# Last part of a four-layer graph network: three of four batches scaled by a product with a diagonal matrix, and the stores moved from GpSimd to SyncE

## The chip, the cores and the metric

The program runs on one core of a Trainium2 chip. A core has five engines that work side by side and meet at semaphores: TensorE (PE in the profile; its weight loads are listed as PEld), VectorE (DVE), ScalarE (ACT), GpSimd (POOL) and SyncE (SP), which here only starts transfers. SBUF is the working memory with 128 partitions; PSUM is the small memory of eight banks into which TensorE writes, one bank being 512 float32 values in each partition. The metric is the device time of one execution in microseconds, and the number that counts is the median of the runs.

## The reference

The program computes four graph layers on `x`, 128 graphs of 128 nodes and 256 features in float32. Each layer is followed by a residual sum and a layer norm. Only the last layer matters here:

```
A_hat = D^-1/2 (adj + I) D^-1/2
agg   = A_hat applied to x, for each of the 128 graphs
h     = relu(batchnorm(agg @ W1.T + b1))          # 512 wide
out   = batchnorm(h @ W2.T + b2)                  # 256 wide
x     = layernorm(x + out)                        # mean and variance over the 256 features, eps 1e-5
```

The batch norms take their mean and variance over all 128 x 128 nodes, so the second one can be applied only when the whole of `h @ W2.T` is there. Applying it is one scale and one shift for each feature. What follows is the residual sum and the layer norm, then the result is stored.

## The kernel before, in words

The 128 graphs are taken in 32 quads of four (`QB` is 4, `NQ` is 32). A quad of the layer's input `x` is kept in DRAM (`x3_dram`), laid out with nodes in the partitions. A quad of `h @ W2.T` stays in SBUF (`outs[q]`, shown as `agg`), and lies the other way round: features in the partitions, in two halves `o` of 128, and in the free dimension four batches of 128 nodes. The two have to be brought together, so the features-first data is turned by TensorE.

The order in which each engine executes its instructions is the order in which the program issues them; the whole part is inside a hand-written schedule, no planner reorders it. [...] Waits come from the data: an instruction waits for what it reads, and for the readers of what it overwrites.

`finish` ends the pass before: it aggregates the statistics of the second batch norm, computes its scale `sc2` and shift `sh2` (L1483 to L1495), applies both to the first quad (`halves`, L1497), and spreads them into two small matrices (`spread`, L1354 and L1355): `diag2`, a diagonal matrix with the scale, and `wide`, with the shift.

The last part (L1522 to L1602) is a software pipeline over the quads. One turn of its loop, for the number `q`, issues in this order:

- `moments(q, 0)`: the first half of quad `q` on VectorE. It adds the turned batches 0 and 1 to `x` in SBUF (L1554), and takes the layer norm's statistics of both (L1557, L1559).
- `scaled(q + 1)`: the next quad's turning. Batches 0 and 1 are scaled and shifted by ScalarE in place (`halves`, L1350, 256 columns for each feature half) and then transposed by TensorE into the PSUM bank `pt[0]` (L1537). Batches 2 and 3 go another way: a product with `diag2` turns and scales them at once into the bank `pt[1]` (L1545), the shift is added to `x` by GpSimd beforehand (L1542), and a product with the identity adds this `x` to the same bank (L1547). So for these two the residual sum is formed in PSUM and VectorE has no add.
- `coefficients(q - 1)`: two small instructions of VectorE that make the reciprocal `rs` (L1564) and minus the mean times `rs`, called `nm` (L1565).
- `apply(q - 1)`: four activations on ScalarE (L1577), one for each batch, which write the normed rows into SBUF; batches 0 and 1 are read from SBUF, 2 and 3 from PSUM. Then the store of the quad, issued by GpSimd (L1583). In the last quad VectorE takes two of the four (L1574), and SyncE and ScalarE store one half each (L1580, L1581).
- the load of a later quad of `x` on SyncE (`load_x3`, L1528).
- `moments(q, 1)`: statistics of batches 2 and 3, read from PSUM, and the square root on ScalarE (L1601).

Twelve buffers hold the quads of `x` (`NB` is 12). Eleven loads are issued ahead of the loop; in turn `q` the load of quad `q + 10` follows, into the buffer of quad `q - 2`, when that quad's store is through. A bank pair `pt` is used again after four quads.

Of the kernel before, what the change touches and what calls it, by code (L numbers as in the profile page):

```python
# [11 lines left out]
AF = mybir.ActivationFunctionType  # L12
# [14 lines left out]
def gnn_stack(ctx: ExitStack, tc: tile.TileContext, x, adj, w_qv_t, a, w_out_t, src, dst,  # L27
# [14 lines left out]
    nc = tc.nc  # L42
    B, N, D = x.shape
    H, DH = a.shape
    E = src.shape[0]
    P = 128
# [3 lines left out]
    QB = 4  # L50
    NQ = B // QB
# [10 lines left out]
    def ctile(shape, name, dtype=F32, pool=const):  # L62
        return pool.tile(shape, dtype, tag=name, name=name)

    def ps(name):
        return psum.tile([P, 512], F32, tag="ps", name=name)
# [6 lines left out]
    ident = ctile([P, P], "ident")  # L73
# [8 lines left out]
    sc2, sh2 = ctile([P, DC], "sc2"), ctile([P, DC], "sh2")  # L82
# [46 lines left out]
    with ExitStack() as phase:  # L129
# [556 lines left out]
        def layer2(k, b, room=None):  # L686
# [84 lines left out]
            pos = [ps("po2").rearrange("p (t d) -> p t d", d=D) for _ in range(2)]  # L771
            yield
            scaled(0)
            v.p4()
            yield
            v.p3()
            po = mix(0)
            scaled(1)
            yield
            mv = norm(0, po)  # L780
# [102 lines left out]
        bias = ctile([P, D], "bias", pool=cst2)  # L883
# [435 lines left out]
    with ExitStack() as phase:  # L1319
# [9 lines left out]
        def buf(name, tag="zbuf"):  # L1329
            return bufs.tile([P, 2 * QB * N], F32, tag=tag, name=name, bufs=NZ if tag == "zbuf" else NT)  # L1330
# [14 lines left out]
        diag2 = ctile([P, DC, P], "diag2", pool=cst)  # L1345
        shift_bc = ctile([P, D], "shift_bc", pool=cst)
        wide = ctile([P, DC, P], "wide", pool=cst)

        def halves(q, o, ag):
            nc.scalar.activation(ag[:, o, :2 * N], ag[:, o, :2 * N], AF.Identity, bias=sh2[:, o:o + 1],  # L1350
                                 scale=sc2[:, o:o + 1])

        def spread(o):
# [3 lines left out]
        with tc.manual_schedule(engines=None):  # L1357
# [114 lines left out]
            def finish(d):  # L1472

                last = ps("x3p")
                product(last, s4, d.b22, True)
                product(d.y, a22, d.t[3], False)
                ag = outs[d.q + 1][:, 0, :]
                nc.vector.tensor_add(ag, last, d.u2)
                nc.vector.bn_stats(st2[:, 0, d.q + 1, :], ag)
                t = bn_t[:, K3:K3 + DC]  # L1480

                def over(o):
                    nc.vector.bn_aggr(t[:, o, 0:2], st2[:, o].rearrange("p q s -> p (q s)"))  # L1483

                over(0)
                nc.vector.bn_stats(st2[:, 1, d.q, :], d.y)
                over(1)
                nc.scalar.activation(t[:, :, 2], t[:, :, 1], AF.Sqrt, bias=eps)
                for o in range(DC):
                    b = bn2[:, 0, o:o + 1]  # L1490
                    nc.vector.tensor_scalar(t[:, o, 3:4], t[:, o, 0:1], b, b, op0=ALU.add, op1=ALU.subtract)
                nc.vector.reciprocal(t[:, :, 2], t[:, :, 2])
                nc.vector.tensor_mul(sc2, bn2[:, 1], t[:, :, 2])
                nc.vector.tensor_mul(t[:, :, 3], t[:, :, 3], sc2)
                nc.vector.tensor_sub(sh2, bn2[:, 2], t[:, :, 3])  # L1495
                for o in range(DC):
                    halves(0, o, outs[0])  # L1497
                nc.scalar.copy(outs[d.q][:, 1, :], d.y)
                for o in range(DC):
                    spread(o)  # L1500
# [21 lines left out]
            x3s, sums, mvs, coefs = {}, {}, {}, {}  # L1522

            NB = NZ + NT

            def load_x3(q):
                x3s[q] = buf(f"x3l{q}", "zbuf" if q % NB < NZ else "tbuf").rearrange("p (b d) -> p b d", b=QB)
                nc.sync.dma_start(x3s[q], x3_dram[q].rearrange("p (b d) -> p b d", b=QB))  # L1528

            def scaled(q):  # L1530
                ag = outs[q]
                pt = [ps("pt3").rearrange("p (b d) -> p b d", d=D) for _ in range(2)]
                for o in range(DC):
                    if q > 0:
                        halves(q, o, ag)
                    for j in range(2):
                        nc.tensor.transpose(pt[0][:, j, o * P:(o + 1) * P], ag[:, o, j * N:(j + 1) * N], ident)  # L1537
                if q == 0:
                    pr = ps("shift_ps")[:, :D]
                    nc.tensor.matmul(pr, ones, wide.rearrange("p o n -> p (o n)"), start=True, stop=True)  # L1540
                    nc.scalar.copy(shift_bc, pr)
                nc.gpsimd.tensor_add(x3s[q][:, 2:, :], x3s[q][:, 2:, :], shift_bc.unsqueeze(1).to_broadcast([P, 2, D]))  # L1542
                for j in range(2):
                    for o in range(DC):
                        nc.tensor.matmul(pt[1][:, j, o * P:(o + 1) * P], ag[:, o, (j + 2) * N:(j + 3) * N], diag2[:, o, :],  # L1545
                                         start=(j == 0 and o == 0), stop=False, skip_group_check=True)
                nc.tensor.matmul(pt[1], ident, x3s[q][:, 2:, :], start=False, stop=True, skip_group_check=True)  # L1547
                sums[q] = pt

            def moments(q, half):  # L1550
                if half == 0:
                    mvs[q] = wk.tile([P, QB, 2], F32, tag="mv3", name="mv3", bufs=3)
                    moments.st = wk.tile([P, QB, 6], F32, tag="st3", name="st3", bufs=2)
                    nc.vector.tensor_add(x3s[q][:, :2, :], x3s[q][:, :2, :], sums[q][0])  # L1554
                src_ = x3s[q][:, :2, :] if half == 0 else sums[q][1]
                for t in range(2):
                    nc.vector.bn_stats(moments.st[:, 2 * half + t, :], src_[:, t, :])  # L1557
                for t in range(2):
                    nc.vector.bn_aggr(mvs[q][:, 2 * half + t, :], moments.st[:, 2 * half + t, :])  # L1559

            def coefficients(q):
                rs = wk.tile([P, QB], F32, tag="rs3", name="rs3", bufs=2)
                nm = wk.tile([P, QB], F32, tag="nm3", name="nm3", bufs=2)
                nc.vector.reciprocal(rs, coefs[q])  # L1564
                nc.vector.scalar_tensor_tensor(nm, mvs[q][:, :, 0], -1.0, rs, op0=ALU.mult, op1=ALU.mult)  # L1565
                coefs[q] = (rs, nm)

            def apply(q):
                rs, nm = coefs[q]
                o_q = out[q * QB:(q + 1) * QB].rearrange("b n d -> n b d")  # L1570
                for i in range(QB):
                    src_ = x3s[q][:, i, :] if i < 2 else sums[q][1][:, i - 2, :]
                    if q == NQ - 1 and i < 2:
                        nc.vector.tensor_scalar(x3s[q][:, i, :], src_, mvs[q][:, i, 0:1], rs[:, i:i + 1],  # L1574
                                                op0=ALU.subtract, op1=ALU.mult)
                    else:
                        nc.scalar.activation(x3s[q][:, i, :], src_, AF.Identity, bias=nm[:, i:i + 1],  # L1577
                                             scale=rs[:, i:i + 1])
                if q == NQ - 1:
                    nc.sync.dma_start(o_q[:, :2], x3s[q][:, :2, :])  # L1580
                    nc.scalar.dma_start(o_q[:, 2:], x3s[q][:, 2:, :])  # L1581
                else:
                    nc.gpsimd.dma_start(o_q, x3s[q])  # L1583

            for q in range(NB - 1):
                load_x3(q)
            scaled(0)
            for q in range(NQ + 1):
                if q < NQ:
                    moments(q, 0)  # L1590
                if q + 1 < NQ:
                    scaled(q + 1)
                if q > 0:
                    coefficients(q - 1)
                    apply(q - 1)
                    if q + NB - 2 < NQ:
                        load_x3(q + NB - 2)
                if q < NQ:
                    moments(q, 1)
                    sd = wk.tile([P, QB], F32, tag="sd3", name="sd3", bufs=2)  # L1600
                    nc.scalar.activation(sd, mvs[q][:, :, 1], AF.Sqrt, bias=eps)  # L1601
                    coefs[q] = sd  # L1602
# [44 lines left out]
```

## Time and profile before

| | |
|---|---|
| median of 9 runs | 3127.83 us (3124.24 to 3130.04) |
| the profiled execution | 3127.5 us |
| its span, first to last instruction | 3125.8 us |
| mean granted TensorE clock | 0.997 |
| busy over the span: TensorE, VectorE, ScalarE, GpSimd | 98%, 74%, 44%, 21% |
| the last part, from the first `halves` to the end of the span | 3013.83 to 3125.8 us |

The profile is one execution. Times are counted from the start of its span. A busy share over the whole span is an average of stages with different limits, so a stage is read by its own windows. In the lists of groups a row gives the line of the kernel, the engine and operation, what it writes and reads, how often, the busy time, the mean of one in nanoseconds, and the idle time of that engine just before, with what ended it. A 512-wide float32 product appears as two records for one matmul of the program, and so do the 128-wide ones with `diag2`; the transposes appear as one.

### The profile page before, as it was taken

The page shows a single profiled execution, that of the slowest core. Times are in us where ns is not written, and L with a number is a line of the kernel's source. Part 1 is how long each engine was busy: PE and PEld are TensorE (multiplying, and loading weights), DVE is VectorE, ACT ScalarE, POOL GpSimd, SP SyncE. Part 2 cuts the span into 40 slices and gives each one's busy share as a digit, 9 for nine tenths or more (in the row PEclk, how much of TensorE's full clock was granted, in tenths as well). Part 3 has the DMA queues.
Part 4 walks back from the last instruction along what each step waited for, and adds up shares of the span by engine and source line. Part 5 has one row for each costly group of instructions (what it writes and reads, how often), then busy time and mean ns, then how long its engine had stood idle before and what let it go on. Part 6 is the DMA issues. An engine that isn't in the chain of part 4 may idle for free. (4 is left out here: it accounts for less than half of the span.)

```text
span 3125.8 us, 39833 instructions
## 1 busy us (share of the span) xinstructions
PE 3075.7 (98%) x14800; PEld 2402.9 (77%) x14800; DVE 2312.7 (74%) x4599; ACT 1374.4 (44%) x2547; POOL 651.6 (21%) x536
## 2 busy tenths in 40 slices
PE   8899999999999999999999999999999999999997
PEld 4688888888888888888888888888888887874444
DVE  8777777777777777777777777777777776457888
ACT  3344443344444444433344444444333444326668
POOL 3311112222211111122222121111222220001135
PEclk9999999999999999999999999999999999999999
DMA  5633233333333332333333333323333331005557
GB/s 181 161 102 92 79 94 109 100 104 109 109 100 84 108 94 77 94 109 102 102 109 109 102 84 107 96 76 94 109 102 102 109 109 42 21 27 202 175 194 278
DMA packets 117473, 340.05 MB, mean 109 GB/s; under 512 B 14880, under 2 KB 51616, under 8 KB 108960
## 3 DMA queue, kind: packets, MB, share of 16 engines
q0 software_dynamic: 44688, 148.40, 19.6%
q1 hardware_dynamic: 70832, 188.18, 17.0%
q8 instruction: 118, 1.93, 0.3%
q10 hardware_dynamic: 1760, 0.92, 0.1%
q14 instruction: 75, 0.61, 0.1%
HBM read 252.00 MB, written 85.46 MB: 108 GB/s over the span
## 5 line engine op out<-in xcount | busy, mean ns | idle before, releaser
L580 PE MATMUL ph<-m,w 128*128 128x256 f32 x2048 | 473.1, 379 | 0.0
L660 PE MATMUL p<-w,h 128*128 128x256 f32 x2048 | 462.8, 379 | 0.0
L580 PEld LDWEIGHTS ph<-m,w 128*128 128x128 f32 x2048 | 386.8, 190 | 77.9 <-issue 14.8
L660 PEld LDWEIGHTS p<-w,h 128*128 128x128 f32 x2048 | 388.9, 190 | 66.4 <-issue 7.9
L336 POOL DMA_INDIRECT zs<-qd,src_idx x120 | 116.3, 969 | 1366.4 <-DMA qd<-qt 1331.5
L580 PE MATMUL ph<-m,w_s 128*128 128x256 f32 x1536 | 357.7, 379 | 0.4 <-DVE h L592 0.4
L580 PEld LDWEIGHTS ph<-m,w_s 128*128 128x128 f32 x1536 | 291.7, 190 | 53.6 <-issue 14.8
L336 POOL DMA_INDIRECT zs<-qd,dst_idx x120 | 189.3, 1577 | 338.8 <-DMA zs<-qd,src_idx 330.0
L586 ACT COPY u<-ph 128x512 f32<-128x512 f32 x128 | 74.6, 583 | 355.0 <-PE ph L580 355.0
L418 POOL DMA_INDIRECT attd<-at,att_idx x128 | 139.9, 1093 | 340.1 <-DMA attd<-at,att_idx 253.3
L596 ACT ACTIVATE h<-h 128x512 f32<-128x512 f32 x192 | 121.0, 630 | 138.8 <-DVE h L592 138.8
L113 ACT ACTIVATE ln_sd<-ln_mv,eps 128x2 f32<-128x2 f32 x192 | 55.9, 291 | 276.4 <-DVE ln_mv L108 276.4
L368 DVE SCALAR_TENSOR_TENSOR zs<-zs 128x1024 f32<-128x1024 f32 x125 | 151.3, 1210 | 8.0 <-DMA zs<-qd,dst_idx 5.3
L370 DVE TENSOR_TENSOR zs<-zs,a_bc 128x1024 f32<-128x1024 f32 x125 | 153.1, 1225 | 4.3
L371 DVE TENSOR_REDUCE scores<-zs 128x16 f32<-128x1024 f32 x125 | 152.5, 1220 | 4.3
L723 ACT COPY x2k<-y 128x384 f32<-128x384 f32 x192 | 91.8, 478 | 143.2 <-PE y L716 113.0
L106 DVE BATCH_NORM_STATS2 ln_st<-xr 128x6 f32<-128x256 f32 x384 | 144.5, 418 | 6.6
L121 DVE TENSOR_SCALAR xr<-xr,ln_mv,ln_rs 128x256 f32<-128x256 f32 x384 | 142.0, 412 | 7.0
L592 DVE TENSOR_TENSOR h<-ph,u 128x512 f32<-128x512 f32 x128 | 86.9, 680 | 71.9 <-PE ph L580 54.6
L437 ACT COPY adc<-ad 128x512 f32<-128x512 f32 x125 | 132.8, 1064 | 8.8 <-DMA ad<-attd 8.8
L684 POOL TENSOR_TENSOR xb<-xr,bias 128x512 f32<-128x512 f32 x64 | 99.1, 1549 | 150.8 <-DVE xr L121 143.7
L537 PE MATMUL pm<-wt_t,h 128*128 128x128 f32 x1024 | 126.9, 277 | 0.0
(359 smaller groups left out, 6083.6 us busy)
## 6 DMA issues: line engine op xcount, KB each, us to landing
ad<-attd SPq DMA_DIRECT2D x32, 1024.0 KB, 4.9
zd<-z SPq DMA_DIRECT2D x31, 1024.0 KB, 7.5
zl<-zd SPq DMA_DIRECT2D x62, 512.0 KB, 3.6
xr<-in_x_dram SPq DMA_DIRECT2D x32, 512.0 KB, 7.2
x3d<-xr SPq DMA_DIRECT2D x32, 512.0 KB, 2.6
x3l<-x3d SPq DMA_DIRECT2D x32, 512.0 KB, 5.5
out_dram<-x3l POOLq DMA_DIRECT2D x31, 512.0 KB, 5.8
xg<-in_x_dram SPq DMA_DIRECT2D x29, 512.0 KB, 3.8
```

The lines of the kernel that those rows point to most:

```text
L106: nc.vector.bn_stats(st[:, i, :], r[:, i, :])
L121: nc.vector.tensor_scalar(r[:, i, :], r[:, i, :], mv[:, i, 0:1], rs[:, i:i + 1], op0=ALU.subtract, op1=ALU.mult)
L336: nc.gpsimd.indirect_dma_start(out=s.z[c], out_offset=None, in_=s.qd, in_offset=bass.IndirectOffsetOnAxis(ap=idx[:, c:c + 1], axis=0), com ...
L368: nc.vector.scalar_tensor_tensor(z, z, SLOPE, z, op0=ALU.mult, op1=ALU.max)
L370: nc.vector.tensor_mul(z3, z3, a_bc.unsqueeze(1).to_broadcast([P, QB, D]))
L371: nc.vector.reduce_sum(s.es[:, c, :], z.rearrange("p (r d) -> p r d", d=DH), axis=AX.X)
L418: nc.gpsimd.indirect_dma_start(out=ad, out_offset=bass.IndirectOffsetOnAxis(ap=att_idx[:, c:c + 1], axis=0), in_=s.at[:, c, :], in_offset= ...
L437: (copy or nc.scalar.copy)(s.adc[:, j * H:(j + 1) * H, :], s.ad.rearrange("p (s r) -> p r s", r=R)[:, j * H:(j + 1) * H, :])
L537: nc.tensor.matmul(pm[:, c // 2, c % 2, :], quads[k].h1[i, c], wt_t, start=True, stop=True)
L580: nc.tensor.matmul(bank[g][:, i].rearrange("p b n -> p (b n)"), wa[:, c, f:f + P], s.m2[:, blk_b, c].rearrange("p b n -> p (b n)"), start= ...
L596: nc.scalar.activation(h, h if src_ is None else src_, AF.Relu)
L660: nc.tensor.matmul(p3[:, t * D:(t + 1) * D], s.h2[f // 2][:, f % 2, j + t, :], w3_sb[:, f, :], start=(f == 0), stop=(f == K2 - 1))
```

## The change

Of each quad, ScalarE scales and shifts only batch 0 and TensorE transposes only batch 0. Batches 1, 2 and 3 take the way of the product with `diag2`: batch 1 into the second half of the bank `pt[0]`, beside the transposed batch 0, and 2 and 3 into `pt[1]` as before. GpSimd adds the shift to three batches of `x`. A further product with the identity, 256 wide, adds `x` of batch 1 to `pt[0]`. VectorE's add covers batch 0 alone, and the statistics and the apply of batch 1 read PSUM. The stores of all quads but the last are issued by SyncE, on the queue that the loads use. The loads ahead of the loop stay at eleven; in the loop, turn `q` loads quad `q + 8`, from turn 3 on, into the buffer of quad `q - 4`.

```diff
--- before.py
+++ after.py
@@ -1347,7 +1347,7 @@
         wide = ctile([P, DC, P], "wide", pool=cst)
 
         def halves(q, o, ag):
-            nc.scalar.activation(ag[:, o, :2 * N], ag[:, o, :2 * N], AF.Identity, bias=sh2[:, o:o + 1],
+            nc.scalar.activation(ag[:, o, :N], ag[:, o, :N], AF.Identity, bias=sh2[:, o:o + 1],
                                  scale=sc2[:, o:o + 1])
 
         def spread(o):
@@ -1533,17 +1533,17 @@
                 for o in range(DC):
                     if q > 0:
                         halves(q, o, ag)
-                    for j in range(2):
-                        nc.tensor.transpose(pt[0][:, j, o * P:(o + 1) * P], ag[:, o, j * N:(j + 1) * N], ident)
+                    nc.tensor.transpose(pt[0][:, 0, o * P:(o + 1) * P], ag[:, o, :N], ident)
                 if q == 0:
                     pr = ps("shift_ps")[:, :D]
                     nc.tensor.matmul(pr, ones, wide.rearrange("p o n -> p (o n)"), start=True, stop=True)
                     nc.scalar.copy(shift_bc, pr)
-                nc.gpsimd.tensor_add(x3s[q][:, 2:, :], x3s[q][:, 2:, :], shift_bc.unsqueeze(1).to_broadcast([P, 2, D]))
-                for j in range(2):
+                nc.gpsimd.tensor_add(x3s[q][:, 1:, :], x3s[q][:, 1:, :], shift_bc.unsqueeze(1).to_broadcast([P, 3, D]))
+                for j in range(1, QB):
                     for o in range(DC):
-                        nc.tensor.matmul(pt[1][:, j, o * P:(o + 1) * P], ag[:, o, (j + 2) * N:(j + 3) * N], diag2[:, o, :],
-                                         start=(j == 0 and o == 0), stop=False, skip_group_check=True)
+                        nc.tensor.matmul(pt[j // 2][:, j % 2, o * P:(o + 1) * P], ag[:, o, j * N:(j + 1) * N],
+                                         diag2[:, o, :], start=(j < 3 and o == 0), stop=False, skip_group_check=True)
+                nc.tensor.matmul(pt[0][:, 1, :], ident, x3s[q][:, 1, :], start=False, stop=True, skip_group_check=True)
                 nc.tensor.matmul(pt[1], ident, x3s[q][:, 2:, :], start=False, stop=True, skip_group_check=True)
                 sums[q] = pt
 
@@ -1551,10 +1551,10 @@
                 if half == 0:
                     mvs[q] = wk.tile([P, QB, 2], F32, tag="mv3", name="mv3", bufs=3)
                     moments.st = wk.tile([P, QB, 6], F32, tag="st3", name="st3", bufs=2)
-                    nc.vector.tensor_add(x3s[q][:, :2, :], x3s[q][:, :2, :], sums[q][0])
-                src_ = x3s[q][:, :2, :] if half == 0 else sums[q][1]
+                    nc.vector.tensor_add(x3s[q][:, 0, :], x3s[q][:, 0, :], sums[q][0][:, 0, :])
                 for t in range(2):
-                    nc.vector.bn_stats(moments.st[:, 2 * half + t, :], src_[:, t, :])
+                    src_ = sums[q][half][:, t, :] if (half, t) != (0, 0) else x3s[q][:, 0, :]
+                    nc.vector.bn_stats(moments.st[:, 2 * half + t, :], src_)
                 for t in range(2):
                     nc.vector.bn_aggr(mvs[q][:, 2 * half + t, :], moments.st[:, 2 * half + t, :])
 
@@ -1569,7 +1569,7 @@
                 rs, nm = coefs[q]
                 o_q = out[q * QB:(q + 1) * QB].rearrange("b n d -> n b d")
                 for i in range(QB):
-                    src_ = x3s[q][:, i, :] if i < 2 else sums[q][1][:, i - 2, :]
+                    src_ = x3s[q][:, 0, :] if i == 0 else sums[q][i // 2][:, i % 2, :]
                     if q == NQ - 1 and i < 2:
                         nc.vector.tensor_scalar(x3s[q][:, i, :], src_, mvs[q][:, i, 0:1], rs[:, i:i + 1],
                                                 op0=ALU.subtract, op1=ALU.mult)
@@ -1580,7 +1580,7 @@
                     nc.sync.dma_start(o_q[:, :2], x3s[q][:, :2, :])
                     nc.scalar.dma_start(o_q[:, 2:], x3s[q][:, 2:, :])
                 else:
-                    nc.gpsimd.dma_start(o_q, x3s[q])
+                    nc.sync.dma_start(o_q, x3s[q])
 
             for q in range(NB - 1):
                 load_x3(q)
@@ -1593,8 +1593,9 @@
                 if q > 0:
                     coefficients(q - 1)
                     apply(q - 1)
-                    if q + NB - 2 < NQ:
-                        load_x3(q + NB - 2)
+
+                    if NB - 1 <= q + NB - 4 < NQ:
+                        load_x3(q + NB - 4)
                 if q < NQ:
                     moments(q, 1)
                     sd = wk.tile([P, QB], F32, tag="sd3", name="sd3", bufs=2)
```

## The prediction

> **What bounds the kernel now.** I read the page first, for where the time lies. TensorE fills the span; the last slices look different.
>
> ```profile
> PE 3075.7 (98%) x14800; PEld 2402.9 (77%) x14800; DVE 2312.7 (74%) x4599; ACT 1374.4 (44%) x2547; POOL 651.6 (21%) x536
> ...
> ACT  3344443344444444433344444444333444326668
> ```
>
> The average says TensorE; ScalarE, idle for most of the kernel, works most in the last part, the only part that the diff touches. So that part is read alone: from 3013.8 us, where the second batch norm's coefficients are ready, to 3125.8. The windows of 5 us of it (columns: window, length, busy of PE, weight loads, VectorE, ScalarE, GpSimd, granted clock, DMA share, GB/s):
>
> ```profile
> 3037.00:3042.00 5.00, 4.77 (x25) 2.61 (x24) 4.54 (x21) 5.00 (x12) 3.47 (x4) 1.00 1.00 361
> ...
> 3062.00:3067.00 5.00, 3.22 (x16) 1.80 (x16) 4.90 (x18) 3.49 (x9) 2.03 (x2) 1.00 0.94 345
> ...
> 3092.00:3097.00 5.00, 4.77 (x23) 2.46 (x23) 4.64 (x21) 5.00 (x13) 3.22 (x4) 1.00 0.97 363
> ```
>
> ScalarE is at 5.00 of 5 in nearly all; the middle row is one of two holes. The groups of the last 262 us, shapes apart, give the pieces (busy, mean ns of one, idle before):
>
> ```profile
> L1542 POOL TENSOR_TENSOR x3l<-x3l,shift_bc 128x512 f32<-128x512 f32 x32 | 40.8, 1279 | 18.5 <-ACT shift_bc L1541 17.9
> ...
> L1350 ACT ACTIVATE agg<-agg,sh,sc 128x256 f32<-128x256 f32 x64 | 35.9, 631 | 0.8 <-DVE sh L1495 0.8
> ...
> L1577 ACT ACTIVATE x3l<-x3l,nm,rs 128x256 f32<-128x256 f32 x62 | 34.8, 630 | 4.1 <-DVE nm L1565 3.5 <-issue 0.6
> ...
> L1577 ACT ACTIVATE x3l<-pt,nm,rs 128x256 f32<-128x256 f32 x64 | 33.3, 591 | 0.5 <-issue 0.5
> ...
> L1583 POOL DMA_DIRECT2D out_dram<-x3l x31 | 23.9, 772 | 38.3 <-POOL x3l L1542 22.8 <-issue 12.4 <-ACT sd L1601 1.9
> ...
> L1554 DVE TENSOR_TENSOR x3l<-x3l,pt 128x512 f32<-128x512 f32 x32 | 22.0, 686 | 1.4 <-issue 1.1 <-PE pt L1537 0.2
> ```
>
> The timeline shows one quad (four batches) and the hole before it:
>
> ```profile
> 3062.69 1.39 DVE L1565 SCALAR_TENSOR_TENSOR nm<-mv,rs 128x4 f32<-128x4 f32 x1
> 3062.77 1.27 POOL L1542 TENSOR_TENSOR x3l<-x3l,shift_bc 128x512 f32<-128x512 f32 x1
> ...
> 3064.12 1.09 ACT L1577 ACTIVATE x3l<-x3l,nm,rs 128x256 f32<-128x256 f32 x2 [1.51 <-DVE nm L1565]
> ...
> 3066.01 0.29 ACT L1601 ACTIVATE sd<-mv,eps 128x4 f32<-128x4 f32 x1
> 3066.20 1.08 ACT L1350 ACTIVATE agg<-agg,sh,sc 128x256 f32<-128x256 f32 x2
> ...
> 3067.18 1.08 ACT L1577 ACTIVATE x3l<-x3l,nm,rs 128x256 f32<-128x256 f32 x2
> ...
> 3068.16 1.01 ACT L1577 ACTIVATE x3l<-pt,nm,rs 128x256 f32<-128x256 f32 x2
> ```
>
> From start to start: two halves 0.98, two applies from SBUF 0.98, two from PSUM 0.90, the root 0.19: 3.05 us a quad, all ScalarE. The hole is the nm instruction (0.16 us elsewhere, 1.39 here): it stands until GpSimd's add ends at 3064.04, and ScalarE waits 1.51 for it. It happens again at 3073.57 (1.30 us). From the first nm (3022.46) to the thirty-first (3117.16): 94.7 us, 30 x 3.055 plus 2 x 1.5.
>
> TensorE with nothing to wait for:
>
> ```profile
> 3070.61 0.60 PE L1537 MATMUL pt<-ident,agg 128*128 128x128 f32 x4
> 3071.04 1.06 PE L1545 MATMUL pt<-diag,agg 128*128 128x128 f32 x8
> 3071.93 1.03 PE L1547 MATMUL pt<-x3l,ident 128*128 128x512 f32 x2
> ```
>
> Four transposes 0.43 (0.107 each), four diagonal products 0.89 (0.223 each), the 512-wide identity product 0.86 of stream (two records of 0.43, as each 512-wide record at L1413): 2.2 us.
>
> **What the Trainium skill says.** *SBUF — State Buffer*, "Who interferes with whom": a VectorE instruction with two SBUF inputs and a GpSimd one that reads SBUF exclude each other; the later stands for the other's whole length. The trace agrees (1.39 above; L1405 lasts 3.18 us beside the 2.35 us GpSimd subtraction, its like L1409 1.20 without). *PSUM — Partial Sum Buffer*, "PSUM bank collisions raise a hardware error": no two engines may use one bank at once, even at different columns; order by bank, not by address. Here every bank is read only after its last write, so this trace can't show it. *ScalarE: Activation LUTs*, "What ACT_TABLE_LOAD costs": 0.833 ns an element; the trace has 0.713 us start to start for 512 (L1367) and 0.49 for 256, 0.87 ns. *DMA: Bandwidth & Descriptors*, "SWDGE vs HWDGE vs iDMA": GpSimd's stores are built by its cores, SP's in hardware; in the trace a store costs POOL 0.77 us, a half store SP 0.39.
>
> **The change, part by part.** Durations of the profiled execution (3127.5 us, span 3125.8, 1.7 around it; median 3127.83).
>
> *ScalarE.* Halves of 128 instead of 256 columns: 2 x (0.49 - 0.11) = 0.76. Apply 1 now reads PSUM: 0.49 + 3 x 0.45 = 1.84. With the root 2.79 of 3.05: 0.26 a quad comes free.
>
> *VectorE.* The add is 256 wide: 0.41 (L548, of that width from PSUM: 410 ns) for 0.69, start to start 0.45 for 0.72. Unstalled work falls from 2.83 (from 3064.00 to 3066.83) to 2.56.
>
> *TensorE.* Two transposes go, two diagonal products and a 256-wide identity product (0.43) come: 0.21 + 1.34 + 0.43 + 0.86 = 2.84. Still below 3.05.
>
> *The new wait.* Bank pt[0] held transposes only, and the add L1554 began after them, beside the products. Now pt[0] also gets two products and the 256-wide product, issued ahead of the add. By the bank rule the add must wait for that last one; without the rule, the second bn_stats still must, because it reads its result. Behind it on VectorE stand bn_stats, bn_aggr and then rs and nm of the quad before; on nm waits ScalarE's apply, behind that its root and the halves of the next quad but one, on them TensorE's transposes. That is a closed chain over two quads. Step by step:
>
> - start of the 256-wide product to the add: 1.12 (the 512-wide one) - 0.43 + 0.05 = 0.74
> - add 0.45, two bn_stats 0.68, bn_aggr 0.22, rs 0.18, nm 0.16 and its signal 0.04: 1.73
> - applies 1.84, root 0.19: 2.03
> - halves, to the end of the second: 1.08 - 2 x 0.11 = 0.86, signal 0.05: 0.91
> - one transpose 0.17, six products 1.34, to the next 256-wide product: 1.51
>
> Sum 6.92 for two quads, 3.46 a quad, above every engine's own work. In the kernel before this chain left the TensorE products out and had slack under ScalarE's 3.05. Bounds: without the bank rule the add and the first bn_stats (0.79) run ahead of it: 6.13, 3.06 a quad. I take 3.46: the page says that the hardware demands it.
>
> 30 x 3.46 = 103.8 against 94.7: +9.1 us.
>
> *Start.* At the stage's half clock four products took 1.91; six take 2.9, from 3015.9 to 3018.7. The first add moves from 3015.76 to after the 256-wide product, 3019.4; the second such product ends near 3022.6, and the first nm comes at 22.6 + 0.45 + 0.68 + 0.22 + 0.18 = 3024.1 for 3022.46: +1.6. The tail after nm 31 (apply, store, 6 us) stays.
>
> *GpSimd.* The add is 768 wide: 1.82 (on the line through 1.28 for 512 and 2.35 for 1024) to 1.92 (in proportion). TensorE waits for it in the first quad alone. The store goes (0.77). With it goes what paced GpSimd: each store waited for an apply, and the add behind it too. Now the adds run as fast as loads are there: eleven are, so from about 3016.7 to 3037 they stand back to back, 100% of the shared port; each nm that falls in waits for an add's end. Bounds: nothing, to a whole add (1.9) on each of some five nm, of which half counts, the chain being two quads long: 0 to 5. I take 0.6 a quad, +3. Later an add follows its load's landing, some 8 us after nm (apply 2.1, issue 0.4, landing 5.5), which is 1.1 after another nm, over by 3.0 of 3.46: mostly clear. Bounds 0 to 0.5 on 19 quads (0 to 10); I take +1. The two holes of before are in the 94.7 already.
>
> *SP.* Store then load each quad: 0.4 + 0.3 us of issue, hidden in 3.46. The store waits for the apply; the load behind it waits for that too, as it did by its place, and for a store three quads older. It is needed seven quads later (24 us) and lands in about 6; were that cover gone, GpSimd's add and then TensorE would stand, by the lateness.
>
> Sum: 9.1 + 1.6 + 3 + 1 = +14.7; 3127.5 + 14.7 = 3142.
>
> **Rivals.** A, as above: 3136 to 3149, chance 0.65. B, the add isn't tied to its bank, or the loop is shorter by as much: 30 x 3.06 = 92 against 94.7, start +1, stalls +4 on average: 3130 (3124 to 3134), 0.14. For it: SBUF halves of one tile are ordered apart here (the first add ran at 3015.76, before GpSimd's at 3017.01). Against it: the PSUM page. C, between back-to-back adds GpSimd keeps the port and the first nm stands until the burst ends: 3037 - 3024 = 13 for the 3 that I counted: 3152 (3149 to 3160), 0.13. Against it: both holes end with the one add; but neither had a second one queued. D, the faster side: the freed ScalarE time is realised, the chain hidden. It decides once the chain is below 2 x 2.84 and nm never meets an add; then TensorE's 2.84 rules: 30 x 2.84 = 85.2, -9.5 + 1.6: 3119.6, 0.06. Against it: VectorE needs the new product before nm by data alone, which gives 3.06. E, stores and loads on one queue starve the adds: the DMA share is 0.9 to 1.0 already; below 0.8 us lateness a quad the lead of seven quads covers it: 3150 and more, 0.02.
>
> **How the numbers follow.** Time 3142 from A. Range 3127 to 3155: A whole, most of B and C, the rest (D, E, the ends) 0.17; A alone 3136 to 3149. 0.2% is 6.3 us, what a measurement of this kernel can tell. Faster (below 3121.5): D and a sliver of B, 0.07. Same: most of B, 0.11. Slower (above 3134.1): A, C, E and B's end, 0.82.
>
> **What would show it.** Right: 3.4 to 3.5 us a quad; ScalarE idle some 0.65 a quad before L1577 on nm; VectorE idle before the add on the identity product; TensorE idle before the transposes on agg; GpSimd's adds back to back until about 3037, nm of 1 to 2 us beside them. Wrong: an add that starts beside the products (B), one nm of 10 us (C), ScalarE full at 2.8 a quad (D), GpSimd waiting for loads with TensorE behind it (E).

## The result, and the profile after

The changed kernel takes 3135.99 us, the median of 9 runs (3133.32 to 3142.18), against 3127.07 us for the kernel before on the same chip. The ratio is 1.0031, with a 95% interval of 1.0023 to 1.0040: slower by 0.3%. The forecast was 3142, range 3127 to 3155, slower with a chance of 0.82.

The profiled execution took 3134.43 us (span 3132.7), 6.9 us more than that of before. The page's first part, and ScalarE's row of the 40 slices:

```profile
PE 3088.7 (99%) x14928; PEld 2425.3 (77%) x14928; DVE 2296.2 (73%) x4599; ACT 1371.0 (44%) x2547; POOL 647.4 (21%) x505
...
ACT  3344433444444444443344444444434344336658
```

TensorE's share rose from 98% to 99%. That does not say that it became the bound: the windows of the last part, with the same columns as those shown of before, say otherwise. Two of them:

```profile
3060.00:3065.00 5.00, 4.61 (x30) 3.47 (x30) 4.11 (x19) 4.00 (x11) 2.81 (x3) 1.00 0.94 322
...
3090.00:3095.00 5.00, 4.61 (x26) 3.07 (x26) 3.81 (x19) 4.00 (x12) 2.83 (x2) 1.00 0.85 296
```

Before, ScalarE had 5.00 of 5. Now no engine is full: TensorE 4.61, VectorE 4.1 or less, ScalarE 4.00, GpSimd 2.8. In the sixteen windows of 5 us from 3035 to 3115 TensorE has 4.61 to 4.95 and ScalarE 3.98 to 4.71; GpSimd alone has 5.00, from 3020 to 3030, in the row of adds with which it begins. When none is full and the work does not stop, the suspect is a closed chain of waits, in which each instruction waits for the one before it and the first for the last, some quads later. The groups of the last 262 us name its joints, in the column behind the second bar (the last row is of the kernel before):

```profile
L1541 POOL TENSOR_TENSOR x3l<-x3l,shift_bc 128x768 f32<-128x768 f32 x32 | 57.5, 1810 | 52.3 <-DMA x3l<-x3d 42.5 <-DMA out_dram<-x3l 4.6 <-PE pt L1544 3.1
...
L1577 ACT ACTIVATE x3l<-x3l,nm,rs 128x256 f32<-128x256 f32 x31 | 18.6, 600 | 17.4 <-DVE nm L1565 16.2 <-POOL x3l L1541 1.2
L1554 DVE TENSOR_TENSOR x3l<-x3l,pt 128x256 f32<-128x256 f32 x32 | 13.5, 421 | 29.0 <-PE pt L1546 29.0
...
L1536 PEld LDWEIGHTS pt<-ident,agg 128*128 128x128 f32 x64 | 8.9, 138 | 40.7 <-ACT agg L1350 40.2 <-issue 0.5
...
L1537 PEld LDWEIGHTS pt<-ident,agg 128*128 128x128 f32 x128 | 13.4, 142 | 42.1 <-ACT agg L1350 40.7 <-issue 1.4
```

VectorE stands 29.0 us before its 32 adds, for the 256-wide identity product; before, it stood 0.2 us there for TensorE. ScalarE stands 16.2 us for nm (3.5 before). TensorE's weight loads stand 40.2 us for the halves, no more than before (40.7); but before, ScalarE itself was full, and now it waits in its turn. So the three stand for each other in a ring. GpSimd waits for loads, but no product waits for GpSimd. One turn of the ring in the timeline:

```profile
3061.63 0.60 PE L1546 MATMUL pt<-x3l,ident 128*128 128x256 f32 x2
...
3062.26 0.42 DVE L1554 TENSOR_TENSOR x3l<-x3l,pt 128x256 f32<-128x256 f32 x1 [0.63 <-PE pt L1546]
...
3063.79 0.16 DVE L1565 SCALAR_TENSOR_TENSOR nm<-mv,rs 128x4 f32<-128x4 f32 x1
...
3063.99 0.60 ACT L1577 ACTIVATE x3l<-x3l,nm,rs 128x256 f32<-128x256 f32 x1 [0.29 <-DVE nm L1565]
...
3066.03 0.87 ACT L1350 ACTIVATE agg<-agg,sh,sc 128x128 f32<-128x128 f32 x2
...
3067.12 1.50 PE L1544 MATMUL pt<-diag,agg 128*128 128x128 f32 x12
...
3068.46 0.60 PE L1546 MATMUL pt<-x3l,ident 128*128 128x256 f32 x2
```

From one 256-wide product to that of two quads later: 3068.46 - 3061.63 = 6.83 us, 3.415 a quad.

Where the 6.9 us of span come from: nm of the first quad to nm of the thirty-first went from 94.7 to 102.98 us (3022.40 to 3125.38), +8.3. From the stage's first halves to the first nm, 8.63 became 9.60, +1.0. The stage began 1.0 earlier (3012.80 for 3013.83), in code that the diff does not touch. And from nm 31 to the end 8.64 became 7.32, -1.3. In sum +6.9. Since the part before the stage scatters by microseconds from execution to execution, the experiments below are compared by their medians and by the time from nm 1 to nm 31.

### The profile page after: what moved, and what is told of

Same layout as the page of the kernel before. It is cut to its first block, busy times and chain, and to the rows that moved or that the text cites. A ratio compares the mean times of both kernels' runs of the same rounds, so it can differ in the third digit from the quotient of the medians.

```text
span 3132.7 us, 40050 instructions
## 1 busy us (share of the span) xinstructions
PE 3088.7 (99%) x14928; PEld 2425.3 (77%) x14928; DVE 2296.2 (73%) x4599; ACT 1371.0 (44%) x2547; POOL 647.4 (21%) x505
```

## The experiments

The theory is that the chain over two quads sets the time, and that the wait of the add for the 256-wide product closes it. The rivals are the queue of SyncE, which now carries loads and stores, and the SBUF port that VectorE and GpSimd share. The kernel before is the other side of every ratio; its median was 3126.9 to 3127.1 in each set.

**The two parts of the change, each alone.** First the scaling alone: the changed kernel with the stores and the loads as before.

```diff
-                    nc.sync.dma_start(o_q, x3s[q])
+                    nc.gpsimd.dma_start(o_q, x3s[q])
...
-                    if NB - 1 <= q + NB - 4 < NQ:
-                        load_x3(q + NB - 4)
+                    if q + NB - 2 < NQ:
+                        load_x3(q + NB - 2)
```

> The changed kernel's scaling alone: stores by GpSimd and loads of quad q + 10 as before the change. Chain theory (VectorE's add waits for the 256-wide product, a closed chain over two quads of 6.83 us): the chain is the same, about 3.4 us a quad, 3134 to 3139 us. Rival queue (the stores in the queue of the loads cost the time): back to 3127, 3.06 a quad. Rival port (adds of GpSimd that run freely hold nm up): the adds are paced by the stores again, 3127 to 3131.

Measured: 3155.32 us, ratio 1.0093 (1.0078 to 1.0109). Every theory missed: the scaling alone costs 28 us, and the chain had been given 7 to 12. Its waits in the last part (us in total, times, longest):

```profile
DVE x3l L1554 <- PE pt L1546: 41.1, 18, 5.0
ACT x3l L1577 <- DVE nm L1565: 35.8, 15, 3.1
PEld pt L1546 <- POOL x3l L1541: 12.6, 16, 1.5
```

The last line is missing in the changed kernel: TensorE's identity products wait for GpSimd's add. (The kernel before has 10.1 us of such waits, while ScalarE is full.) The timeline shows why.

```profile
3065.55 0.77 POOL L1583 DMA_DIRECT2D out_dram<-x3l  x1 [3.37 <-issue]
...
3066.34 1.81 POOL L1541 TENSOR_TENSOR x3l<-x3l,shift_bc 128x768 f32<-128x768 f32 x1
...
3068.20 0.70 PE L1546 MATMUL pt<-x3l,ident 128*128 128x256 f32 x2 [1.31 <-POOL x3l L1541]
...
3068.94 0.42 DVE L1554 TENSOR_TENSOR x3l<-x3l,pt 128x256 f32<-128x256 f32 x1 [3.25 <-PE pt L1546]
```

GpSimd's store waits for its quad's apply, and the add of a later quad stands behind it. From the store 0.79 us to the add, 1.86 to the product, 0.74 to VectorE's add, 1.52 to nm (3070.46), 0.30 to the apply (3070.76), 1.85 for its four, 0.65 to the next store but one (3073.26): 7.71 us for this turn over two quads, a second closed chain. Late in this trace two quads take 7.98 (nm from 3118.99 to 3126.97); there nm takes 0.51 us for 0.26 in the turn shown, since it stands longer for a GpSimd add. The loads went back to their old places in this run too and were not tried alone, but no add of GpSimd waits for a load in its last part; the ring goes through the store.

Then the stores and loads alone, in the kernel before, the same lines the other way round.

> The kernel before with the stores on SyncE and the later loads alone; the scaling stays at two batches. Chain theory: ScalarE stays the bound at 3.05 us a quad; the 512-wide adds now run back to back at the start and then with the loads, so that some nm wait up to 1.3 us, while the two holes of before may go: 3124 to 3131. Rival queue: slower by the whole loss, 3134 to 3138. Rival port: clearly slower, 3131 and more.

Measured: 3126.02 us, ratio 0.9997 (0.9988 to 1.0005), no difference. The queue of SyncE costs nothing here, and moving the stores gains nothing by itself; nm stalls oftener (418 ns in the mean for 236), but ScalarE waits only 3.4 us for it. So the parts do not add: the move of stores and loads is worth nothing alone and 3155.32 - 3135.99 = 19 us beside the scaling, because it takes the store out of GpSimd's queue.

**Which wait closes the chain.** The transposed batch 0 gets a bank of its own, three banks a quad, so that VectorE's add no longer shares one with the products; the shift's product moves into that bank's second half.

```diff
-                pt = [ps("pt3").rearrange("p (b d) -> p b d", d=D) for _ in range(2)]
+                b0, *pt = [ps("pt3").rearrange("p (b d) -> p b d", d=D) for _ in range(3)]
...
-                    nc.tensor.transpose(pt[0][:, 0, o * P:(o + 1) * P], ag[:, o, :N], ident)
+                    nc.tensor.transpose(b0[:, 0, o * P:(o + 1) * P], ag[:, o, :N], ident)
...
-                    nc.vector.tensor_add(x3s[q][:, 0, :], x3s[q][:, 0, :], sums[q][0][:, 0, :])
+                    nc.vector.tensor_add(x3s[q][:, 0, :], x3s[q][:, 0, :], sums[q][2][:, 0, :])
```

> The changed kernel with the transposed batch 0 in a PSUM bank of its own, three banks a quad, nothing else moved. Chain theory: add and first statistics run ahead of the 256-wide product, the chain is shorter by 0.8 us in two quads (6.05), 3.03 a quad: 3136 less 30 x 0.39, 3124 (3121 to 3128), and VectorE no longer idles before the add. Rival TensorE (the added products are the bound): no change, 3136. Rivals queue and port: no change, 3136.

Measured: 3130.57 us (3125.05 to 3137.55), ratio 1.0013 (1.0007 to 1.0020). The wait of the add is gone; the second bn_stats now waits, but 9.9 us in all. Of the 8.9 us of loss 5.4 are gone, not all as expected. A stall of nm, a whole add long, shows in the timeline (of an execution of 3125.05 us, the shortest of the runs):

```profile
3060.35 1.80 POOL L1541 TENSOR_TENSOR x3l<-x3l,shift_bc 128x768 f32<-128x768 f32 x1 [0.74 <-ACT agg L1350]
3060.36 1.82 DVE L1565 SCALAR_TENSOR_TENSOR nm<-mv,rs 128x4 f32<-128x4 f32 x1
```

**How much of it is the port.** The changed kernel, and then the one with its own bank, without GpSimd's adds (one line of `scaled`).

```diff
-                nc.gpsimd.tensor_add(x3s[q][:, 1:, :], x3s[q][:, 1:, :], shift_bc.unsqueeze(1).to_broadcast([P, 3, D]))
```

> The changed kernel without GpSimd's adds: the shift of batches 1 to 3 is left out of the result, everything else is there. Chain theory: nothing holds nm up any more, but the chain stays, 3.4 a quad: 3133 to 3136. Rival port: the loss goes, 3126 to 3129.

> The transposed batch 0 in a bank of its own, and GpSimd's adds left out (the shift of batches 1 to 3 is missing from the output). If what the own bank left of the loss (3.5 us, with a wide spread) is nm standing beside GpSimd's adds, this takes it away: 3123 (3121 to 3126), with a narrow spread. If it is the rest of the chain, 3129 to 3131.

Measured: 3134.57 us without the adds, ratio 1.0023 (1.0014 to 1.0033); with the bank besides, 3121.55, ratio 0.9981 (0.9971 to 0.9990). In both, nm takes 0.16 us every time. Two nm that lie two quads apart, first with the shared bank, then with the own one:

```profile
3082.02 0.16 DVE L1564 SCALAR_TENSOR_TENSOR nm<-mv,rs 128x4 f32<-128x4 f32 x1
...
3088.85 0.16 DVE L1564 SCALAR_TENSOR_TENSOR nm<-mv,rs 128x4 f32<-128x4 f32 x1
```

```profile
3060.85 0.16 DVE L1564 SCALAR_TENSOR_TENSOR nm<-mv,rs 128x4 f32<-128x4 f32 x1
...
3066.90 0.16 DVE L1564 SCALAR_TENSOR_TENSOR nm<-mv,rs 128x4 f32<-128x4 f32 x1
```

Two quads still take 6.83 us with the shared bank: the chain alone, with the port idle, holds nearly the whole loss. With the own bank they take 6.05, as expected. So GpSimd's adds cost 1.4 us with the shared bank and 9 us with the own bank: the long chain had covered them.

**Shortening the chain in other ways.** The reciprocal and nm of the quad before are issued ahead of the add; or between the first and second bn_stats; or there and with the own bank (in the last two, those of the last quad stay where they were). The edit of the first:

```diff
+                if q > 0:
+                    coefficients(q - 1)
                 if q < NQ:
                     moments(q, 0)
                 if q + 1 < NQ:
                     scaled(q + 1)
                 if q > 0:
-                    coefficients(q - 1)
                     apply(q - 1)
```

> rs and nm of the quad before are issued ahead of the next quad's add, so they no longer stand behind the wait for the 256-wide product; nothing else is changed. Chain theory: the chain over two quads is opened; what is left are loops of one quad (statistics, root, rs, nm, add, statistics: about 2.9 to 3.07 us), so 30 x 3.0 for 30 x 3.43: 3124 (3121 to 3129). Rival, TensorE's own work or the shared port is the bound: 3136, as with the change.

> rs and nm between the first and the second bn_stats, the bank shared as in the change. Chain theory: one bn_stats and the bn_aggr (0.56 us) leave the chain of 6.83, which becomes 6.27, 3.14 a quad: 30 x 0.28 = 8.4 us less than with the change: 3127.5 (3125 to 3130). Rival, the chain is not what sets the quad: 3136.

> The transposed batch 0 in a bank of its own, and rs and nm of the quad before between the first and the second bn_stats. Chain theory: no closed chain is longer than TensorE's own 2.84 us a quad, so TensorE is the bound at 2.84 to 2.95: 3119 (3116 to 3123), faster than both. Port rival: with three batches added by GpSimd, nm still stands beside its adds and carries into a shorter chain: 3125 to 3131, as with the bank alone.

Measured: 3130.53 (ratio 1.0011, 1.0002 to 1.0019), 3131.56 (1.0014, 1.0007 to 1.0021) and 3124.04 (0.9990, 0.9983 to 0.9996; 3119.16 to 3130.14). All three are faster than the change, none by as much as the chain theory expected; the third lies between its two ranges. Where nm is not stalled the quads are about as short as worked out: 3.04 (nm 3108.02 to 3111.06), 6.30 for two (3066.89 to 3073.19, expected 6.27), and 2.80 (3061.41 to 3064.21, expected 2.84). What is missing is in nm. Its group in the third of them:

```profile
L1567 DVE SCALAR_TENSOR_TENSOR nm<-mv,rs 128x4 f32<-128x4 f32 x32 | 23.3, 727 | 1.1
```

23.3 us where 32 x 0.163 = 5.2 are work: 18 us of standing. From nm 1 to nm 31 it took 97.99 us, where 30 quads at TensorE's own 2.84 would be 85.2; this profiled execution, 3130.14 us, is the longest of its runs. In the changed kernel the group has 6.8 us.

**Taking nm off the port.** The third of these, with the means and variances of all quads but the last in the unused half of the transposed batch's bank, so that nm has one operand in PSUM and one in SBUF. (The root then reads PSUM too.)

```diff
-                    mvs[q] = wk.tile([P, QB, 2], F32, tag="mv3", name="mv3", bufs=3)
+                    mvs[q] = (sums[q][2][:, 1, :2 * QB].rearrange("p (b s) -> p b s", s=2) if q < NQ - 1
+                              else wk.tile([P, QB, 2], F32, tag="mv3", name="mv3", bufs=3))
```

> The own bank and the middle place of rs and nm, and besides the means and variances (all quads but the last) are written into the unused half of the transposed batch's bank, so nm reads one operand from PSUM and one from SBUF instead of two from SBUF. Port theory: nm no longer stands beside GpSimd's adds (0.16 us throughout) and the quad takes what TensorE needs, 2.85 us: 5 us less than with the own bank and no adds, 3116 to 3119. Rival, nm's stall is not tied to its two SBUF operands: 3124, as with the two edits alone.

Measured: 3115.57 us (3114.22 to 3119.09), ratio 0.9965 (0.9951 to 0.9978): faster than both kernels, by 11.5 and by 20.4 us. Its nm group:

```profile
L1568 DVE SCALAR_TENSOR_TENSOR nm<-pt,rs 128x4 f32<-128x4 f32 x31 | 5.0, 162 | 1.1
```

And from its timeline, GpSimd's twelve back-to-back adds and an nm in their midst:

```profile
3018.11 21.32 POOL L1541 TENSOR_TENSOR x3l<-x3l,shift_bc 128x768 f32<-128x768 f32 x12 [17.45 <-ACT shift_bc L1540]
...
3027.26 0.16 DVE L1568 SCALAR_TENSOR_TENSOR nm<-pt,rs 128x4 f32<-128x4 f32 x1
```

GpSimd's adds take as long as ever (1819 ns in the mean), and nm no longer stands for them. From nm 1 to nm 31: 3024.41 to 3110.03, 85.6 us, 2.85 a quad. A window of 10 us, with the columns as above, has TensorE and ScalarE without a gap:

```profile
3060.00:3070.00 10.00, 10.00 (x67) 8.21 (x66) 9.51 (x39) 10.00 (x26) 6.94 (x4) 1.00 1.03 368
```

Of the two TensorE sets the pace. In the run before, where nm was free for a few quads, nm came every 2.81 us at the end while TensorE's identity products stayed 2.85 apart (3111.94, 3114.79, 3117.64): ScalarE can go faster, its own work being 2.79 a quad by the prediction, and TensorE without a gap does not.

The same edit to the kernel before, with a bank for each quad's means and variances:

```diff
+                    mvs[q] = (ps("mv3")[:, :2 * QB].rearrange("p (b s) -> p b s", s=2) if q < NQ - 1
+                              else wk.tile([P, QB, 2], F32, tag="mv3", name="mv3", bufs=3))
```

> The kernel before with its means and variances in a PSUM bank of their own for each quad. Port theory: the two holes of 1.5 us on ScalarE go, and nothing else changes: 3124 (3123 to 3126). Rival, a third bank for each quad shortens the rotation of the banks and TensorE waits: over 3128.

Measured: 3123.19 us, ratio 0.9987 (0.9981 to 0.9994). nm takes 0.16 us throughout, and most quads 3.02 (3.06 before). Two of 3.80 remain (nm from 3057.87 to 3061.67, and from 3067.70 to 3071.51), so the two holes are halved, from 1.6 us to 0.8 each, and not gone. The trace shows what is left of them: in both, a store of GpSimd comes late (at 3055.44 and 3065.28), the add behind it is late too, and TensorE's identity product waits 0.94 and 1.02 us for that add. The kernel before has the same late stores (3056.65 and 3067.53) and the same waits of the product (0.90 and 0.98). There nm came 0.8 us late because of them, fell into the next add, and stood. So the holes, which the prediction put down to nm, are nm's in half. Why the store is late is not known.

## Why the prediction was right, and where its sizes were off

**The chain: right, and nearly to the number.** Predicted 6.92 us for two quads, measured 6.83. By its steps, in the turn shown above: from the product to the add 0.63 us (predicted 0.74); add to apply 1.73 (1.73); applies and root 2.04 (2.03); halves to the second transpose (3066.95) 0.92 (0.91); from there to the next product 1.51 (1.51). The one that differs was carried over from a wider product. Over 30 quads: 15 x 6.83 = 102.5 against 94.7, +7.8 for +9.1. The runs without GpSimd's adds and with the own bank show that this chain is the cause: with the port idle the loss stays, with the add's wait gone more than half of it goes.

**The bank: right as a wait, open as hardware.** The add does wait for a product that writes only the other half of its bank, 29.0 us in 32 times, as the Trainium skill led me to expect (*PSUM — Partial Sum Buffer*, "PSUM bank collisions raise a hardware error": keep engines apart by bank, not by address). But the program orders it so with its own semaphores. That the chip would demand it was not tried.

**nm at the port: this term failed in size.** I gave +3 to the row of adds at the start and +1 to the rest; the 30 quads took 102.98 us, of which the chain is 102.5, so +0.5 is left for both. The run without GpSimd's adds says the same: 102.57 us, 0.4 less. GpSimd's adds did stand back to back, eleven in 19.49 us, as said. The error was in charging each of some five quads an average stall of 0.6 on top of the chain. An nm that falls into a row of adds waits to the end of one, and these ends come every 1.77 us; the chain's 3.415 a quad is just short of two of them, 3.54. So the first quads fall into step with the adds and lose 0.13 each, and not half an add:

```profile
3025.25 0.80 DVE L1565 SCALAR_TENSOR_TENSOR nm<-mv,rs 128x4 f32<-128x4 f32 x1
...
3029.29 0.30 DVE L1565 SCALAR_TENSOR_TENSOR nm<-mv,rs 128x4 f32<-128x4 f32 x1
...
3032.72 0.41 DVE L1565 SCALAR_TENSOR_TENSOR nm<-mv,rs 128x4 f32<-128x4 f32 x1
```

These end at 3026.05, 3029.59 and 3033.13, 3.54 apart each time. The first nm's of the own bank and of the three runs with rs and nm moved also end 3.53 or 3.54 apart while the row of adds lasts, though their quads take 2.80 to 3.15 when nm is free: the shorter the chain, the more a stall costs. After the row the adds follow the loads. Most start 0.9 to 1.6 us after an nm (nm at 3063.79, the add at 3064.72), near the 1.1 predicted, and end before the next; three of the later nm's still stand, and take 0.26 to 0.44 us.

**Start and tail.** The start cost 1.0 for the 1.6 predicted. The tail was said to stay and became 1.3 us shorter. It is 8.6 us in the three profiles where GpSimd issues the stores (before, the scaling alone, and before with its means in PSUM) and 7.3 to 7.4 in those with SyncE's that I compared (the change, the stores alone, the change without the adds, the own bank, the fastest kernel): it goes with the store's move. About 1.0 us of it lies in the very last transfer, a half quad that ScalarE issues in every kernel: from issue to landing it takes 3.4 us in the kernel before and 2.4 in the changed one. Why it lands sooner is not settled.

**What was not priced.** The move of the stores was counted only as the loss of what had paced GpSimd. Its main effect is that a second chain, store, add, product, add, nm, apply, store, is not there. That the forecast did not suffer was luck: the change has both parts, so the chain that was not seen is one that it does not have. The expectation for the scaling alone missed by 16 us and more.

**The rivals.** B, add not tied to its bank: wrong for this kernel. Its 3130 is near the 3130.57 of the own bank, and its 3.06 a quad near the 3.03 measured without the adds; but it put the stalls at 4 us, where leaving out GpSimd's adds gave 9 back, so the total agrees by luck. C, one nm of 10 us: wrong, the longest in the profile is 0.80; a waiting VectorE instruction gets in between two back-to-back adds. D, TensorE's 2.84 the bound: wrong here, but its condition, chain hidden and nm never at the port, is what the fastest kernel meets; there TensorE sets 2.85 us a quad, and the kernel takes 3115.57, where D said 3119.6. E, loads that starve the adds: wrong, no product waits for GpSimd's add.

## What to carry to other kernels

Before work is shifted from a full engine to others, write down the ring of waits that goes through the new order, over as many loop turns as it spans, and compare that with the engines' own work; here it gave 6.92 us for two quads, and 6.83 were measured, where every engine alone had 5.7 or less. Two parts of a change that look separate should be tried apart and together: one was worth nothing alone and 19 us beside the other. A stall that costs little while a chain is long comes back when the chain is cut, so the cure, a small operand in PSUM in place of SBUF, is worth trying along with the cut and not after it.

## What the runs showed of the hardware

- VectorE's small two-operand instruction stands for GpSimd's add only when both operands are in SBUF. With one of them in PSUM it took 0.16 us in each of 31 quads, among the same 128x768 adds beside which it took up to 1.82. The Trainium skill (*SBUF — State Buffer*, "Who interferes with whom") states both sides: two SBUF inputs contend with a GpSimd instruction that reads SBUF, one at most does not. The traces agree, and show what it is worth here: 8.5 us between 3124.04 and 3115.57.
- Back-to-back GpSimd adds of 1.81 us follow one another every 1.77 us by the profile, and a VectorE instruction that waits gets its turn at the end of the add that is running, and not at the end of the row: every nm of more than 0.2 us, in eight profiles, ended within 0.04 us of an add's end.
- GpSimd's add of 768 columns takes 1.81 us, on the line through 1.28 for its add of 512 and 2.35 for its subtraction of 1024.
